# Attention and feed-forward kernel on one Trainium2 core: the order of its last outputs, the reading of its flag and the place of its short path

## The chip, the core and the metric

The kernel runs on one core of a Trainium2 chip. The core has five engines with instruction queues of their own: TensorE (PE, with its weight loads as PEld), VectorE (DVE), ScalarE (ACT), GpSimd (POOL) and SyncE (SP). [...] DMA transfers are issued here by SP, ACT and POOL. [...] The metric is the device time of one launch in microseconds (us); lower is better.

## What is computed

The input `x` has 32 batches of 64 rows of 512 columns. A cross-attention with 8 heads of 64 columns is added to it, and then a gated feed-forward with integer weights of 16 levels, each with a scale and a zero point for every group of 128 rows:

```
x = x + xattn(layernorm(x), ctx, ctx, Wq, bq, Wk, bk, Wv, bv, Wo, bo)
gate = silu(layernorm(x) @ ((gate_w - gate_z) * gate_s))    # 512 -> 1792
up   =      layernorm(x) @ ((up_w   - up_z)   * up_s)       # 512 -> 1792
x = x + (gate * up) @ ((down_w - down_z) * down_s)          # 1792 -> 512
```

All outputs are float32, 4 MB in all.

## The kernel before, in words

Two batches make a pair of 128 rows, so there are 16 pairs. Four pairs make a block, and there are four blocks, numbered `t` = 0 to 3. Each block's feed-forward works on columns: `hTh` and `hTl` hold the normalised rows turned over, split into a high and a low part so that each product is made of two matmuls. The 1792 inner columns are cut into 14 pieces (`FC`, index `f`). `gate_up(t, f)` makes one piece of gate and up in PSUM, with scalings on ACT (L643) between the groups, then silu (L646) and the product `h` (L649, DVE), which POOL splits into `hh` and `hl` (L659, L660). `down(t, f)` multiplies that piece into four PSUM tiles `pd`, one for each 128 output columns `l`, and DVE adds each to a running sum `y` in SBUF (L691). For the very last piece, ACT and DVE split `h` instead of POOL (L656, L657), and the last two pieces are accumulated in the same PSUM tiles after a scaling on ACT (L685).

**Rounds.** The main loop at L904 runs 118 rounds: 28 for a block and 6 more, since `down` lags six rounds (`LAG`) behind. In each round, `t, k = divmod(r, 28)`, and the loop traces one step of the gate and up lanes, some steps of the next block's attention, two steps of `down`, and side work. A scheduler orders what is traced, by its own estimate of when operands are ready and by trace order as priority. `tc.issue_after(ins)` pins what is traced inside it behind `ins` on the engine of `ins`. `tc.manual_schedule(engines={PE})` keeps PE's instructions in the order traced and together; `tc.high_priority()` inside it puts the rest of such a group ahead once its first instruction has been taken. `Attention.in_order` uses these two for the attention's groups of matmuls.

**Outputs of blocks 0 to 2.** `finish(t)` (L695) has four steps, two for each half of a block. One step loads the residual rows `r` of two pairs back from DRAM (L700, SP, 512 KB). The next turns `y` back into rows with eight transposes on PE into the two PSUM banks of `two_banks` (L705), adds `r` on DVE (L708) and sends two pairs of outputs (L709, SP, 512 KB). `two_banks` has one buffer, which the attention, `finish`, the bounds check and the last outputs share. The main loop takes a step of `finish(t)` in the rounds `k` = 7, 9 and 11 of block `t+1`, and the fourth at `k` = 5 of the block after that. Before the change, the fourth step of `finish(2)` therefore falls into round 117, the last one.

**Outputs of block 3.** `finish_last` (L712) transposes all four pairs (L720) into four PSUM banks, `py[0]` to `py[3]`, of which the last two are the banks of `two_banks`. DVE adds the residual `x` to pairs 0, 1 and 2 (L724). For pair 3, ACT copies the bank to SBUF as `y_last` (L727) and POOL adds the residual (L728). The four sends (L729, 256 KB each) are issued by SP for pairs 0 and 2 and by ACT for pairs 1 and 3. ACT's instructions are traced in the order: send of pair 1, copy of pair 3, send of pair 3.

**The flag.** The split-and-scale arithmetic is exact enough only within bounds on the scales and weights. `check_bounds` computes a one-word `flag` (L758) in round 106, at 406.7 us of the profiled execution. At L939, every engine loads the flag into a register and branches: non-zero leads to a long way, which computes the feed-forward again in plain form. With these inputs the flag is zero and the long way is never run. In the program before, the block of the long way stands right behind the branch, the block of the short way behind it, and the end of the program last. The long way has 286 instructions on SP, 469 on ACT, 509 on DVE, 2087 on PE and 29 on POOL. The short way only brings the semaphores to the values that the long way would have left: one wait-and-add on each of PE, DVE, ACT and POOL, for the engine's own work, and eight on SP, one for each semaphore that counts landed DMAs. So SP waits there until the last output has landed. The end of the program is twelve more waits on SP, and barriers of all engines.

Of the kernel before, what the change touches and what calls it, by code (L numbers as in the profile page):

```python
# [9 lines left out]
F32 = mybir.dt.float32  # L10
# [16 lines left out]
def kernel(  # L27
# [41 lines left out]
    nc = tc.nc  # L69
    B, D, L = x.shape  # L70
    I = gate_w.shape[1]
    P = 128
# [3 lines left out]
    LC = L // P  # L76
    NPAIR = B // 2
    PB = 4
    NBLK = NPAIR // PB
    TB = PB * P  # L80
    SET = 2
# [4 lines left out]
    o_rows = out.rearrange("(n b) d l -> (b d) n l", b=2)  # L86
# [7 lines left out]
    flag = keep.tile([1, 1], I32, tag="flag", name="flag")  # L94
    ident = keep.tile([P, P], F32, tag="ident", name="ident")
# [18 lines left out]
    with ExitStack() as fast:  # L114
# [204 lines left out]
        def top_steps():  # L319
# [9 lines left out]
            for piece in pieces:  # L329
# [3 lines left out]
                nc.gpsimd.tensor_tensor(total[:, :n], total[:, :n], square[:, :n], ALU.add)  # L333
                yield


        class Attention:

# [27 lines left out]
                flat = src.rearrange("p i l -> p (i l)")  # L366
                return flat.rearrange("p (n h d) -> p n h d", h=2, d=D)

            @contextmanager
            def in_order(self):  # L370


                with tc.manual_schedule(engines={mybir.EngineType.PE}), ExitStack() as ahead:
                    yield lambda: ahead.enter_context(tc.high_priority()) if self.n > 1 else None


            def stats(self):
# [215 lines left out]
        FINISH_AT = 7, 11  # L593
# [27 lines left out]
        h_hi, h_lo, y_sb, pd_two = {}, {}, {}, {}  # L621
# [73 lines left out]
        def finish(t: int):  # L695

            for a in range(0, PB, SET):
                p = t * PB + a
                r = rows.tile([P, SET, L], F32, tag="r", name=f"r_{p}")
                nc.sync.dma_start(r, x1_dram[:, p : p + SET, :])  # L700
                yield
                py = two_banks(f"py_{p}")
                for i in range(SET):
                    for l in range(LC):
                        nc.tensor.transpose(  # L705
                            py[:, i, ts(l, P)], y_sb[t, l][:, ts(a + i, P)], ident
                        )
                nc.vector.tensor_tensor(r, py, r, ALU.add)  # L708
                nc.sync.dma_start(o_rows[:, p : p + SET, :], r)  # L709
                yield  # L710

        def finish_last():  # L712

            t = NBLK - 1
            py = [ps_gu.tile([P, CW], F32, tag="gu", name=f"py_last_{i}") for i in range(2)]
            two = two_banks("py_last")
            py += [two[:, 0, :], two[:, 1, :]]
            for l in range(LC):
                for i in range(PB):
                    nc.tensor.transpose(py[i][:, ts(l, P)], y_sb[t, l][:, ts(i, P)], ident)  # L720
            for i in range(PB):
                r = xs[(t * PB + i) // SET][:, i % SET, :]
                if i < PB - 1:
                    nc.vector.tensor_tensor(r, py[i], r, ALU.add)  # L724
                else:
                    y = hid.tile([P, TB], F32, tag="g", name="y_last", bufs=2)
                    nc.scalar.copy(y, py[i])  # L727
                    nc.gpsimd.tensor_tensor(r, y, r, ALU.add)  # L728
                (nc.scalar if i % 2 else nc.sync).dma_start(o_rows[:, t * PB + i, :], r)  # L729


        def check_bounds():
# [57 lines left out]
        with (  # L790
# [9 lines left out]
            for p in range(PB):  # L800
                j, i = divmod(p, SET)
# [96 lines left out]
        ROUNDS = 2 * FC  # L898
        LAG = 6
        done = object()  # L900
        bounds = check_bounds()
        BOUNDS_AT = 3 * ROUNDS + FC + LC
        with ExitStack():
            for r in range(NBLK * ROUNDS + LAG):  # L904
                t, k = divmod(r, ROUNDS)
                if k == 0:
                    attend = attention_steps(t + 1) if t + 1 < NBLK else iter(())
                if k == LAG and t > 0:
                    finishing = finish(t - 1)
                next(lanes[0], done)  # L910
                advance(attend)
                if r >= LAG:
                    advance(downs)
                if r >= 2:
                    next(lanes[1], done)

                with ExitStack() as behind:
                    for ins in newest.values():
                        behind.enter_context(tc.issue_after(ins))
                    if r in (5, 13):  # L920
                        load_weights(*wide[(5, 13).index(r) + 2])
                    if r < ROUNDS:
                        advance(weights, 2 if r < 4 else 1 + r % 2)
                    else:
                        advance(tops, 1 + (r % 4 == 3))
                    if k in FINISH_AT or k + 2 in FINISH_AT:
                        advance(finishing)
                if r >= LAG:
                    advance(downs)
                if r == ROUNDS:  # L930
                    with tc.issue_after(newest["DVE"]):
                        last_quotients()
                if r in (BOUNDS_AT, BOUNDS_AT + 4):
                    with tc.issue_after(newest["DVE"]):
                        next(bounds, None)
        finish_last()


    with tc.If(nc.values_load(flag, min_val=0, max_val=1) != 0), ExitStack() as slow:  # L939
        const = slow.enter_context(tc.tile_pool(name="f_const", bufs=1))  # L940
        work = slow.enter_context(tc.tile_pool(name="f_work", bufs=2))
        ps = slow.enter_context(
            tc.tile_pool(name="f_ps", bufs=2, space=bass.MemoryType.PSUM)
        )
        wg = const.tile([P, KT, I], F32, tag="wg", name="f_wg")
        wu = const.tile([P, KT, I], F32, tag="wu", name="f_wu")
        wd = const.tile([P, FC, L], F32, tag="wd", name="f_wd")

        def dequantise(dst: bass.AP, w: bass.AP, z: bass.AP, s: bass.AP, n: int, name: str):
            w_sb = work.tile([P, CW], I32, tag="w", name=f"f_w_{name}")  # L950
            z_sb = work.tile([P, CW], I32, tag="z", name=f"f_z_{name}")
            s_sb = work.tile([P, CW], F32, tag="s", name=f"f_s_{name}")
            nc.sync.dma_start(w_sb[:, :n], w)
            nc.sync.dma_start(z_sb[:, :n], z.partition_broadcast(P))
            nc.sync.dma_start(s_sb[:, :n], s.partition_broadcast(P))

            nc.vector.tensor_tensor(dst, w_sb[:, :n], z_sb[:, :n], ALU.subtract)
            nc.vector.tensor_tensor(dst, dst, s_sb[:, :n], ALU.mult)

        for at, n in wide:  # L960
            c = slice(at, at + n)
            for g in range(KT):
                dequantise(wg[:, g, c], gate_w[ts(g, P), c], gate_z[g, c], gate_s[g, c], n, f"g{g}{at}")
                dequantise(wu[:, g, c], up_w[ts(g, P), c], up_z[g, c], up_s[g, c], n, f"u{g}{at}")
        for f in range(FC):
            dequantise(wd[:, f, :], down_w[ts(f, P), :], down_z[f, :], down_s[f, :], L, f"d{f}")

        for p in range(NPAIR):
            xp = work.tile([P, L], F32, tag="x", name=f"f_x_{p}")
            nc.sync.dma_start(xp, x1_dram[:, p, :])  # L970
            xn = work.tile([P, L], F32, tag="xn", name=f"f_xn_{p}")
            mv, rs = ln_stats(xp, f"s{p}")
            ln_scale(rs)
            ln_apply(xn, xp, mv, rs)
            ph = ps.tile([P, KT, P], F32, tag="ph", name=f"f_ph_{p}")
            for c in range(KT):
                nc.tensor.transpose(ph[:, c, :], xn[:, ts(c, P)], ident)
            hT = work.tile([P, KT, P], F32, tag="hT", name=f"f_hT_{p}")
            nc.scalar.copy(hT, ph)
            h_sb = work.tile([P, FC, P], F32, tag="h", name=f"f_h_{p}")  # L980
            for f in range(FC):
                pg = ps.tile([P, 2, P], F32, tag="gu", name=f"f_gu_{p}_{f}")
                for m, w in enumerate((wg, wu)):
                    for k in range(KT):
                        nc.tensor.matmul(
                            pg[:, m, :], w[:, k, ts(f, P)], hT[:, k, :], start=(k == 0), stop=(k == KT - 1)
                        )
                g_sb = work.tile([P, P], F32, tag="g", name=f"f_g_{p}_{f}")
                nc.scalar.activation(g_sb, pg[:, 0, :], AF.Silu)
                nc.vector.tensor_tensor(h_sb[:, f, :], g_sb, pg[:, 1, :], ALU.mult)  # L990
            pd = ps.tile([P, L], F32, tag="pd", name=f"f_pd_{p}")
            for f in range(FC):
                nc.tensor.matmul(pd, h_sb[:, f, :], wd[:, f, :], start=(f == 0), stop=(f == FC - 1))
            nc.vector.tensor_tensor(xp, pd, xp, ALU.add)
            nc.sync.dma_start(o_rows[:, p, :], xp)
# [52 lines left out]
```

## Time and profile before

| what | value |
|---|---|
| median of 4 runs | 442.38 us (441.8 to 444.09) |
| the profiled execution's own time | 442.91 us |
| its span, from first to last instruction | 440.8 us |
| time outside the span | 2.1 us |
| busy share of PE, DVE, ACT, POOL | 92%, 75%, 69%, 64% |
| mean granted TensorE clock | 0.990 |
| the last step of `finish(2)` on DVE (L708) | starts 429.23, takes 1.21 |
| sends of the four last pairs | 432.24, 432.84, 433.44, 435.40 |

"Busy" counts arithmetic; waits, register loads, branches and DMA issues are not in it. Matmuls overlap, so PE can be called busy while it still waits a little. Lines such as L939 in the profile are lines of the kernel before.

### The profile page before, as it was taken

To read this page: it belongs to the slowest core of one execution; us is meant where nothing else is said; L and a number is where in the kernel's file an instruction comes from. 1 tells how busy PE (TensorE), PEld (TensorE's weight loads), DVE (VectorE), ACT (ScalarE), POOL (GpSimd) and SP (SyncE) were. 2 spreads that over 40 slices of the span, in tenths; PEclk is the share of its full clock that TensorE was granted. 3 is DMA by queue.
4 is the path that set the end of the run, shared out by engine and by line. 5 is a ranking of instruction groups with operands and counts; after the bars stand their busy time and mean duration, and the time that the engine had idled before them with its cause. 6 is when DMAs were issued, how large, how long until landed. Compare 5 with 4: busy or idle time off the path is not lost.

```text
span 440.8 us, 10355 instructions
## 1 busy us (share of the span) xinstructions
PE 406.7 (92%) x4191; PEld 313.1 (71%) x4191; DVE 330.3 (75%) x514; ACT 306.2 (69%) x469; POOL 280.0 (64%) x292
## 2 busy tenths in 40 slices
PE   4768988989889999999999999989999999999991
PEld 3646656757668776877777787867778888887870
DVE  4988577897789875895779885895868646668682
ACT  2243887565967579766988589657887787777750
POOL 4384948754944546575788668765787878873311
PEclk9999989999999999999999999999999999999997
DMA  7299549197011200411010111400010022100004
GB/s 212 67 311 371 183 127 303 49 263 239 2 49 48 98 2 0 144 51 51 0 50 2 49 38 60 145 0 3 0 50 1 1 90 62 41 1 0 1 2 150
DMA packets 20912, 36.55 MB, mean 83 GB/s; under 512 B 1832, under 2 KB 7416, under 8 KB 20856
## 3 DMA queue, kind: packets, MB, share of 16 engines
q1 hardware_dynamic: 14056, 24.20, 16.6%
q0 software_dynamic: 6192, 11.01, 8.7%
q8 instruction: 35, 0.57, 0.6%
q10 hardware_dynamic: 608, 0.59, 0.4%
q14 instruction: 21, 0.17, 0.1%
HBM read 27.37 MB, written 8.42 MB: 81 GB/s over the span
## 4 chain that ended last, share of the span: by engine, by line
PE 51%; POOL 16%; DVE 13%; issue 11%; ACT 5%; DMA 2%; POOLq 0%; ACTq 0%; DVEq 0%
PE pu L633 14%; PE pg L633 14%; PE pd L678 7%; PE pd L681 6%; POOL hl L660 4%; POOL squares L333 3%; DVE y L691 3%; POOL squares L331 3%; POOL hh L659 2%; DVE xn_set L112 2%; DVE nd L301 2%; ACT pu L643 1%; POOL q_e_set L503 1%; ACT pg L643 1%; DMA x<-in_x_dram 1%
## 5 line engine op out<-in xcount | busy, mean ns | idle before, releaser
L691 DVE SCALAR_TENSOR_TENSOR y<-pd,s_all,y 128x512 f32<-128x512 f32 x204 | 150.2, 744 | 42.9 <-PE pd L681 39.9
L643 ACT ACTIVATE pg<-pg,s_q 128x512 f32<-128x512 f32 x168 | 111.6, 666 | 67.1 <-PE pg L633 65.7
L643 ACT ACTIVATE pu<-pu,s_q 128x512 f32<-128x512 f32 x168 | 111.1, 663 | 8.3 <-PE pu L633 7.3
L659 POOL CAST hh<-h 128x512 fp32r<-128x512 f32 x55 | 35.9, 652 | 97.7 <-DVE h L649 95.9
L678 PE MATMUL pd<-hh,nd 128*128 128x512 f32 x224 | 93.1, 416 | 3.0 <-DVE y L691 2.3
L633 PE MATMUL pg<-hTh,ng 128*128 128x512 f32 x224 | 90.3, 403 | 3.1 <-DVE hTl L576 1.6
L633 PE MATMUL pu<-hTh,nu 128*128 128x512 f32 x224 | 90.8, 406 | 1.5 <-POOL nu L310 1.4
L633 PE MATMUL pg<-hTl,ng 128*128 128x512 f32 x224 | 89.2, 398 | 0.0
L633 PE MATMUL pu<-hTl,nu 128*128 128x512 f32 x224 | 89.0, 397 | 0.0
L681 PE MATMUL pd<-hl,nd 128*128 128x512 f32 x224 | 88.6, 396 | 0.0
L660 POOL TENSOR_TENSOR hl<-h,hh 128x512 fp32r<-128x512 f32 x55 | 71.7, 1303 | 4.3
L649 DVE SCALAR_TENSOR_TENSOR h<-pu,s_all,g 128x512 f32<-128x512 f32 x56 | 41.8, 747 | 30.0 <-ACT g L646 18.1
L333 POOL TENSOR_TENSOR squares<-squares 128x512 f32<-128x512 f32 (+1 forms) x46 | 55.1, 1198 | 1.6
L678 PEld LDWEIGHTS pd<-hh,nd 128*128 128x128 f32 x224 | 42.0, 188 | 19.3 <-DVE y L691 5.9
L633 PEld LDWEIGHTS pg<-hTh,ng 128*128 128x128 f32 x224 | 42.4, 189 | 17.5 <-issue 3.0
L633 PEld LDWEIGHTS pu<-hTh,nu 128*128 128x128 f32 x224 | 42.3, 189 | 15.9 <-POOL nu L310 2.1
L633 PEld LDWEIGHTS pg<-hTl,ng 128*128 128x128 f32 x224 | 42.4, 189 | 9.4
L633 PEld LDWEIGHTS pu<-hTl,nu 128*128 128x128 f32 x224 | 42.4, 189 | 9.3
L646 ACT ACTIVATE g<-pg,s_all 128x512 f32<-128x512 f32 x56 | 38.9, 695 | 14.2 <-PE pg L633 12.7
L681 PEld LDWEIGHTS pd<-hl,nd 128*128 128x128 f32 x224 | 42.1, 188 | 7.7
L310 POOL TENSOR_TENSOR nu<-nu,z 128x512 fp32r<-128x512 f32 (+1 forms) x16 | 17.3, 1084 | 1.6 <-DMA nu<-in_L_ffn_up_w_dram 1.6
L310 POOL TENSOR_TENSOR ng<-ng,z 128x512 fp32r<-128x512 f32 (+1 forms) x16 | 16.5, 1040 | 1.8 <-DMA z<-z_dram 1.8
(293 smaller groups left out, 467.3 us busy)
## 6 DMA issues: line engine op xcount, KB each, us to landing
c_set<-in_ctx_dram SPq DMA_DIRECT2D x6, 512.0 KB
x<-in_x_dram SPq DMA_DIRECT2D x6, 512.0 KB
z<-z_dram SPq DMA_DIRECT2D x6, 512.0 KB
ng<-in_L_ffn_gate_w_dram POOLq DMA_DIRECT2D x3, 1024.0 KB, 6.1
nu<-in_L_ffn_up_w_dram POOLq DMA_DIRECT2D x3, 1024.0 KB, 8.0
x_dram<-x SPq DMA_DIRECT2D x6, 512.0 KB
r<-x_dram SPq DMA_DIRECT2D x6, 512.0 KB
out_dram<-r SPq DMA_DIRECT2D x6, 512.0 KB
```

The costliest lines, as they stand in the source:

```text
L310: nc.gpsimd.tensor_tensor(piece, piece.bitcast(F32), z16[:, m, g, :], ALU.subtract)
L331: nc.gpsimd.tensor_tensor(square[:, :n], piece, piece, ALU.mult)
L333: nc.gpsimd.tensor_tensor(total[:, :n], total[:, :n], square[:, :n], ALU.add)
L633: nc.tensor.matmul(acc, w[:, g, ts(f, P)], half[:, g, :], start=(g == 0 and half is hi), stop=(g == KT - 1 and half is lo), skip_group_che ...
L643: nc.scalar.activation(acc, acc, AF.Copy, scale=by)
L646: nc.scalar.activation(g_sb, acc, AF.Silu, scale=by)
L649: ins = nc.vector.scalar_tensor_tensor(h_sb, acc, by, g_sb, ALU.mult, ALU.mult)
L659: nc.gpsimd.tensor_copy(hh, h_sb)
L660: ins = nc.gpsimd.tensor_tensor(hl, h_sb, hh.bitcast(F32), ALU.subtract)
L678: nc.tensor.matmul(pd, w, h_hi[t, f], start=(t, f) != LAST, stop=False, skip_group_check=True)
L681: nc.tensor.matmul(pd, w, h_lo[t, f], start=False, stop=True, skip_group_check=True)
L691: ins = nc.vector.scalar_tensor_tensor(y, pd, by, y, ALU.mult, ALU.add)
```

## The change

There are four edits. (1) The group context of `Attention.in_order` becomes a free function `in_one_piece`, and `finish` puts its eight transposes into it, with priority after the first. (2) A constant `LAST_OUT` = 3·28 + 11 + 2 = 97 makes the main loop take the fourth step of `finish(2)` in round 97 instead of round 117. (3) In `finish_last`, ACT's copy of pair 3 is traced ahead of everything but the transposes, and ACT's sends are pinned behind it. (4) The flag is loaded ahead of `finish_last`; ACT's and POOL's instructions of `finish_last` are pinned behind their loads of it, and the conditional block is told to prefer the false arm, the short way, as the block that follows the branch.

```diff
+        @contextmanager
+        def in_one_piece(rush: bool = True):
+            with tc.manual_schedule(engines={mybir.EngineType.PE}), ExitStack() as ahead:
+                yield lambda: ahead.enter_context(tc.high_priority()) if rush else None
...
-            @contextmanager
             def in_order(self):
-                with tc.manual_schedule(engines={mybir.EngineType.PE}), ExitStack() as ahead:
-                    yield lambda: ahead.enter_context(tc.high_priority()) if self.n > 1 else None
+                return in_one_piece(self.n > 1)
...
                 py = two_banks(f"py_{p}")
-                for i in range(SET):
-                    for l in range(LC):
-                        nc.tensor.transpose(
-                            py[:, i, ts(l, P)], y_sb[t, l][:, ts(a + i, P)], ident
-                        )
+                with in_one_piece() as first_taken:
+                    for i in range(SET):
+                        for l in range(LC):
+                            nc.tensor.transpose(
+                                py[:, i, ts(l, P)], y_sb[t, l][:, ts(a + i, P)], ident
+                            )
+                            first_taken()
...
+            y = hid.tile([P, TB], F32, tag="g", name="y_last", bufs=2)
+            copied = nc.scalar.copy(y, py[PB - 1])
             for i in range(PB):
                 r = xs[(t * PB + i) // SET][:, i % SET, :]
                 if i < PB - 1:
                     nc.vector.tensor_tensor(r, py[i], r, ALU.add)
                 else:
-                    y = hid.tile([P, TB], F32, tag="g", name="y_last", bufs=2)
-                    nc.scalar.copy(y, py[i])
                     nc.gpsimd.tensor_tensor(r, y, r, ALU.add)
-                (nc.scalar if i % 2 else nc.sync).dma_start(o_rows[:, t * PB + i, :], r)
+                with tc.issue_after(copied.ins):
+                    (nc.scalar if i % 2 else nc.sync).dma_start(o_rows[:, t * PB + i, :], r)
...
+        LAST_OUT = (NBLK - 1) * ROUNDS + FINISH_AT[1] + 2
...
-                    if k in FINISH_AT or k + 2 in FINISH_AT:
+                    if k in FINISH_AT or k + 2 in FINISH_AT or r == LAST_OUT:
                         advance(finishing)
...
-        finish_last()
+        n_traced = len(nc.cur_bb.bb.instructions)
+        other = nc.values_load(flag, min_val=0, max_val=1)
+        with ExitStack() as behind:
+            for ins in nc.cur_bb.bb.instructions[n_traced:]:
+                if ins.engine in (mybir.EngineType.Activation, mybir.EngineType.Pool):
+                    behind.enter_context(tc.issue_after(ins))
+            finish_last()
...
-    with tc.If(nc.values_load(flag, min_val=0, max_val=1) != 0), ExitStack() as slow:
+    with tc.If(other != 0, preferred_fallthrough_block=False), ExitStack() as slow:
```

## The prediction

> **What bounds the kernel now.** I read the page first, then windows of the last rounds, the timeline of the last ten microseconds, and the instructions of the flag's line. The page:
>
> ```profile
> span 440.8 us, 10355 instructions
> PE 406.7 (92%) x4191; PEld 313.1 (71%) x4191; DVE 330.3 (75%) x514; ACT 306.2 (69%) x469; POOL 280.0 (64%) x292
> ...
> q8 instruction: 35, 0.57, 0.6%
> q14 instruction: 21, 0.17, 0.1%
> ```
>
> PE bounds the run, so work moved about beside PE is free and work moved onto PE is not. The two instruction queues fetch code: 35 packets of 16 KB on q8, 21 of 8 KB on q14. The windows show PE full in block 3, with room on DVE and POOL:
>
> ```profile
> 380.00:400.00 20.00, 20.00 (x87) 15.78 (x86) 14.93 (x30) 15.64 (x26) 13.52 (x14) 1.00 0.00 1
> 400.00:420.00 20.00, 20.00 (x88) 15.72 (x86) 14.13 (x21) 14.80 (x25) 7.09 (x8) 1.00 0.00 0
> ```
>
> The columns after the window are its length and then busy time of PE, PEld, DVE, ACT and POOL. The change acts on the tail:
>
> ```profile
> 429.23 1.21 DVE L708 TENSOR_TENSOR r<-py,r 128x1024 f32<-128x1024 f32 x1
> 430.36 0.74 DVE L691 SCALAR_TENSOR_TENSOR y<-pd,s_all,y 128x512 f32<-128x512 f32 x1
> 431.52 1.89 DVE L724 TENSOR_TENSOR x<-py_last,x 128x512 f32<-128x512 f32 x3 [0.42 <-PE py_last L720]
> 432.24 1.53 SPq L729 DMA_DIRECT2D out_dram<-x  x2
> 433.44 0.59 ACT L727 COPY y_last<-py_last 128x512 f32<-128x512 f32 x1 [5.91 <-DVE x L724]
> 434.11 1.26 POOL L728 TENSOR_TENSOR x<-y_last,x 128x512 f32<-128x512 f32 x1 [12.52 <-DMA out_dram<-x]
> 435.40 0.34 ACTq L729 DMA_DIRECT2D out_dram<-x  x1
> ...
> L939 SPq EVENT_SEMAPHORE  x8: 17/17/17, 437.0 to 438.8; - x8
> L939 PEldq COMPARE_BRANCH  x1: 4357/4357/4357, 432.2 to 432.2; - x1
> L939 SPq COMPARE_BRANCH  x1: 45/45/45, 433.8 to 433.8; - x1
> L939 POOLq COMPARE_BRANCH  x1: 54/54/54, 435.0 to 435.0; - x1
> L939 POOLq EVENT_SEMAPHORE  x1: 17/17/17, 435.4 to 435.4; - x1
> L939 ACTq COMPARE_BRANCH  x1: 58/58/58, 436.3 to 436.3; - x1
> L939 ACTq EVENT_SEMAPHORE  x1: 17/17/17, 439.9 to 439.9; - x1
> ```
>
> The reader is to see two things. DVE's add for block 2 (L708) stands between block 3's sums and their last member. And a branch over the long way is dear: SP branches at 433.82 and does its next instruction at 436.98, 3.16 us later; ACT goes from 436.32 to 439.85 (3.53), PE takes 4.36, while POOL, whose long way has only 29 instructions, takes 0.36 (435.04 to 435.40). On SP this lies beside the outputs' flight. The trace's semaphore events put the last landing of pair 3 at 438.69. SP takes it at 438.71 and needs 0.13 for two more waits, then twelve waits of the program's end, 0.062 each. The last of those stands 0.31 for ACT's late semaphore; with ACT in time, the end would be 440.52 in place of 440.81. So ACT's branch is worth 0.29, and the landing rules.
>
> **The block 2 step, moved from round 117 to 97.** Eight transposes start 0.109 apart (260.10 to 260.86 in an earlier group). Rounds 89 and 93 stand at 355.75 and 367.82 (transposes), so a round is 3.02 and round 97 is near 379.9. PE is full there: +0.87. DVE's 1.21 fits into its 5.07 idle us of that window; with no such cover it adds up to 1.21. The residual load (L700) is issued at 373.1, nearly 7 us ahead, where a 512 KB send took 2.8 (430.47 to 433.26): 0; if late, the add and the send wait, not PE. The moved send on SP has only the flag's load (406.8) behind it: 0. In the tail L708 goes: the three sums from 427.20 end at 429.31, so the last `y` starts at 429.23, as L708 did, not 430.36: −1.13. The twelve transposes that waited for L708's bank are done by then. Net so far −0.26: last `y` ends at 430.84 instead of 431.10. Keeping the other groups together costs nothing: all five already run 0.11 apart. If priority puts a group ahead of its free bank, PE stands; the nearest row is PE's wait for L708's bank, 0.69.
>
> **The copy first.** Pair 3's last transpose ends 0.71 after the last `y` (431.81), so ACT can copy at 431.60 (430.84 + 0.71 + 0.05) instead of 433.44. With 0.59, a hop of 0.07 and POOL's 1.26 the add ends at 433.52 and the send leaves at 433.55, not 435.40: −1.85. POOL's add now runs beside DVE's; `hl` took 1.30 under a busy DVE, so +0.04 at most. Behind the copy on ACT stand the sends of pairs 1 and 3; pair 1 waits for DVE until 432.58 anyway, after the copy ends at 432.19: 0. The other sends move by −0.26, to 431.98, 432.58 and 433.18.
>
> **The flag early.** ACT's load (0.47) falls between 427.5, its last scaling, and 431.6; POOL's (0.90) after 421.6: 0, without cover +0.47 and +0.90. PE's (0.96) and DVE's (0.82) are not pinned; I leave them last, as now. Ahead of PE's transposes it would cost +0.96 at most. SP's already stands at 406.8.
>
> **The short way behind the branch.** The long way must then stand elsewhere. The only other place that leaves the rest in order is between the short way and the program's end, so the short way ends in a jump over the long way, as far as the jump of before. The stall is not removed; it moves behind the short way's waits. For PE, DVE and ACT that stays hidden: ACT sends at 433.55, is through 0.34 later, and with 3.53 is done by 437.6. For SP it does not: its jump now comes after the last landing. The price is bounded by POOL's 0.36 and PE's 4.36; I take SP's own row, 3.16, the same engine and distance.
>
> [...]
>
> **Landing.** Without laggards, 15 of 16 parts of pairs 0, 1 and 2 landed by 434.27, 434.95 and 435.64, some 2.03 after the send and 0.68 apart; so pair 3 would be in at 436.06 (431.98 + 2.03 + 3 × 0.68). But each pair's last part was late (436.54, 437.22, 437.81) while code packets were fetched (433.9 to 435.2). The fetches stay among the sends, as PE and DVE jump right after their work. Pair 2 took 4.38 from send to landing: 437.56 now, and pair 3 0.64 behind it, 438.20. By pair 3's own row, 3.30, it is 436.85. I take the middle, 437.5; ends 436.06 and 438.2.
>
> **Sum.** Landing 437.5, two waits and the take-up 0.15, jump 3.16, twelve waits 0.74, hand-over 0.06, closing barriers 0.87 (439.94 to 440.81): 442.5 against 440.8, so +1.7. The profiled execution took 442.91, 2.1 around its span, and lies 0.53 above the median; on its own time I get 444.6, on the median's scale 444.1.
>
> **The rivals.** *First, no jump on SP's path* (faster): the end follows the short way directly, or the target is already fetched. For it: POOL's 0.36 shows a cheap jump. Against it: the distance. Then 437.5 + 0.15 + 0.74 + 0.06 + 0.87 = 439.3 with laggards, 437.9 without (no jumps, no fetches among the sends): −1.5 to −2.9, taken at −2.6, 439.8. It decides where the stall falls under 3.16 − 1.7 = 1.4. *Second, the moved step disturbs block 3*: DVE's 1.21 delays `y` sums, PE waits for `pd` banks (8 such waits, 5.9 us in all, before), or a group stands for its bank: 0.69 to 1.9 on top, 444.8 to 446.0, 445.5 with the jump. Against it: after L708 at 369.04 the windows show no gap on PE. *Third, the jump stays but laggards go*: landing 436.06, +0.2, 442.6; it needs the fetches to miss the sends.
>
> **How the numbers follow.** 0.5% is 2.2 us, about what a measurement of this kernel can tell from no change. The jump with its landing between the two ends: 0.70 (third rival included with 0.15), own range 442.4 to 445.3 from landing 436.06 to 438.2 and a stall of 3.1 to 3.5; about a third of it lies above 444.6. First rival 0.17, range 439.3 to 441.0, two thirds of it below 440.2. Second rival 0.13, nearly all above 444.6. Faster 0.12; slower 0.23 + 0.11 = 0.34; within 0.54. For 8 in 10 the range takes in both: 439.5 to 445.4.
>
> **What would show it.** Right: the flag line's eight SP waits now start soon after 433.8, as soon as SP branches, and end with the last landing; then some 3 us without any SP instruction before the closing waits; ACT's copy starts ahead of both its sends, near 431.6; no L708 after 382. Wrong: closing waits directly behind the last landing (first rival), or PE gaps near 380 (second). The prediction fails by most if the place of the long way is not as I argue.

## The result, and the profile after

| | median | range | runs |
|---|---|---|---|
| before | 443.24 us | 441.22 to 444.98 | 78 |
| after | 444.38 us | 442.56 to 446.56 | 52 |

The ratio of after to before is 1.0031, with a 95% interval of 1.0023 to 1.0040: slower by 1.0 to 1.8 us, which is within the 0.5% that the prediction called no change. The profiled execution of after took 445.28 us, its span is 443.18, so 2.10 lies around the span as before.

In the change, line 708 became 713 (DVE's add), 709 became 714, 720 became 725, 724 became 732, 727 became 728, 728 became 734, 729 became 736, 649 became 652 and 691 became 694. Line 939 was split: the loads of the flag are at 946, the branch and the short way at 954. The end of the program is 1058.

The top of the page of after, the lines that answer those of before:

```profile
span 443.2 us, 10359 instructions
PE 406.2 (92%) x4191; PEld 311.5 (70%) x4191; DVE 330.8 (75%) x514; ACT 306.0 (69%) x469; POOL 280.3 (63%) x292
...
q8 instruction: 35, 0.57, 0.5%
q14 instruction: 22, 0.17, 0.1%
```

Nothing was added to or taken from the arithmetic; the span is 2.4 us longer with the same work, and 0.83 of that is drift, which is taken off below. The windows of block 3 after:

```profile
380.00:400.00 20.00, 20.00 (x91) 16.22 (x90) 14.99 (x28) 14.62 (x24) 13.39 (x13) 1.00 0.07 27
400.00:420.00 20.00, 20.00 (x87) 15.47 (x86) 14.60 (x23) 15.49 (x26) 7.64 (x8) 1.00 0.00 1
```

The first window has 91 matmuls in place of 87, and a DMA share of 0.07 in place of 0.00. That is the moved step with its transposes and its send. PE has no gap; the step pushes the rest of block 3 back by its own length.

To compare ends, one correction is needed. The executions drift apart in the first 140 us: after's products `h` (L652) are 0.80 later than before's at 125.4 us and still 0.83 at 380.4, and the executions in the table below stand between −0.7 and +1.3 us to the one of before. I read the drift at one of DVE's products `h` in block 3, and the cost of the moved step at the next one. Before, then after:

```profile
380.40 0.75 DVE L649 SCALAR_TENSOR_TENSOR h<-pu,s_all,g 128x512 f32<-128x512 f32 x1 [0.50 <-ACT g L646]
...
384.60 0.75 DVE L649 SCALAR_TENSOR_TENSOR h<-pu,s_all,g 128x512 f32<-128x512 f32 x1 [0.50 <-ACT g L646]
```

```profile
381.24 0.75 DVE L652 SCALAR_TENSOR_TENSOR h<-pu,s_all,g 128x512 f32<-128x512 f32 x1 [0.49 <-ACT g L649]
...
386.32 0.75 DVE L652 SCALAR_TENSOR_TENSOR h<-pu,s_all,g 128x512 f32<-128x512 f32 x1 [0.49 <-ACT g L649]
```

The first `h` is 0.83 later, the next 1.72. So the moved step costs 0.88 (1.715 less 0.834). Times "on before's scale" below have the drift taken off.

In the views a "q" behind an engine's name (SPq, ACTq) marks register loads, branches, semaphore waits and DMA issues. Arithmetic of the same engine can lie beside them: DVE's load of the flag before (0.82 from 431.9) lies beside its three adds (431.52 to 433.41). The timeline of the tail of after:

```profile
429.54 2.15 DVE L694 SCALAR_TENSOR_TENSOR y<-pd,s_all,y 128x512 f32<-128x512 f32 x3
...
431.08 1.53 PE L725 MATMUL py_last<-ident,y 128*128 128x128 f32 x12 [0.41 <-DVE y L694]
432.32 1.89 DVE L732 TENSOR_TENSOR x<-py_last,x 128x512 f32<-128x512 f32 x3 [0.64 <-PE py_last L725]
432.65 0.59 ACT L728 COPY y_last<-py_last 128x512 f32<-128x512 f32 x1 [3.38 <-PE py_last L725]
433.04 1.53 SPq L736 DMA_DIRECT2D out_dram<-x  x2
433.31 1.27 POOL L734 TENSOR_TENSOR x<-y_last,x 128x512 f32<-128x512 f32 x1 [10.01 <-ACT y_last L728]
433.64 2.04 ACTq L736 DMA_DIRECT2D out_dram<-x  x2
```

The copy now runs beside DVE's adds, and ACT has issued its second send 1.07 us after it began at 434.61. On before's scale pair 3 leaves at 433.78 instead of 435.40. Now the instructions of the branch's line, and SP's closing waits, of after (durations in ns, then the first and last start in us):

```profile
L954 SPq EVENT_SEMAPHORE  x8: 17/17/17, 434.7 to 438.9; - x8
L954 PEldq COMPARE_BRANCH  x2: 90/2062/4033, 432.3 to 432.8; - x2
...
L954 SPq COMPARE_BRANCH  x2: 38/44/49, 434.6 to 438.9; - x2
L954 ACTq COMPARE_BRANCH  x2: 38/48/57, 435.7 to 435.9; - x2
```

```profile
L1058 SPq EVENT_SEMAPHORE  x14: 17/28/28, 441.5 to 443.1; - x14
```

Each engine now has two branches at this line: one into the short way, which costs SP 0.10 (434.62 to 434.72), and one out of it, over the long way. SP's eight waits begin right behind the first, at 434.72, and end behind the last landing (438.70 by the trace's semaphore events; SP takes it at 438.72). SP's second branch is at 438.92, its next instruction at 441.55. For those 2.63 us no engine does any work. PE's jump (432.81 to 436.90), DVE's (434.34 to 437.88) and ACT's (435.89 to 438.50) lie ahead of that, hidden.

So the change sends the last pair 1.62 us sooner, the last landing comes only 0.83 sooner (437.87 on before's scale against 438.69), and the end comes 4.48 behind the landing instead of 2.11: −0.83 + 2.37 = +1.54 in the traces. What became of the missing 0.8 of the earlier send is a question for the experiments.

### The profile page after: what moved, and what is told of

It reads as the page before. It is cut to its first block, busy times and chain, and to the rows that moved or that the text cites. A ratio compares the mean times of both kernels' runs of the same rounds, so it can differ in the third digit from the quotient of the medians.

```text
span 443.2 us, 10359 instructions
## 1 busy us (share of the span) xinstructions
PE 406.2 (92%) x4191; PEld 311.5 (70%) x4191; DVE 330.8 (75%) x514; ACT 306.0 (69%) x469; POOL 280.3 (63%) x292
## 4 chain that ended last, share of the span: by engine, by line
PE 48%; POOL 18%; DVE 12%; issue 11%; DMA 5%; ACT 4%; POOLq 0%; SPq 0%; DVEq 0%; ACTq 0%
PE pu L636 13%; PE pg L636 13%; PE pd L681 7%; PE pd L684 6%; POOL hl L663 4%; DMA nd<-in_L_ffn_down_w_dram 4%; POOL squares L333 3%; DVE y L694 3%; POOL squares L331 3%; POOL hh L662 2%; DVE nd L301 2%; DVE xn_set L112 1%; POOL q_e_set L506 1%; DMA x<-in_x_dram 1%; POOL nu L310 1%
## 5 line engine op out<-in xcount | busy, mean ns | idle before, releaser
L652 DVE SCALAR_TENSOR_TENSOR h<-pu,s_all,g 128x512 f32<-128x512 f32 x56 | 41.9, 747 | 29.3 <-ACT g L649 18.6
```

What stands on the lines that cost most here:

```text
L652: ins = nc.vector.scalar_tensor_tensor(h_sb, acc, by, g_sb, ALU.mult, ALU.mult)
```

## The experiments

All ratios are to runs of the kernel before on the same chip, taken together with it. Each experiment has 12 runs, except "no long way" (6) and "long first, short jump" (11). The other columns are read from one trace of each kernel, on before's scale and each rounded on its own, in the order run.

| kernel | ratio | 95% interval | cost in block 3 | pair 3 sent | last landing | end − landing | end |
|---|---|---|---|---|---|---|---|
| before | 1 | | | 435.40 | 438.69 | 2.11 | 440.81 |
| after | 1.0031 | 1.0023 to 1.0040 | 0.88 | 433.78 | 437.87 | 4.48 | 442.35 |
| long way first | 1.0011 | 0.9990 to 1.0032 | 0.88 | 433.75 | 437.92 | 2.61 | 440.53 |
| short way first, alone | 1.0042 | 1.0023 to 1.0062 | 0 | 435.41 | 437.94 | 4.38 | 442.32 |
| block 2's step, alone | 0.9992 | 0.9971 to 1.0012 | 0.88 | 435.35 | 438.62 | 1.83 | 440.44 |
| copy first, alone | 0.9988 | 0.9968 to 1.0008 | 0 | 433.80 | 438.52 | 1.83 | 440.35 |
| short jump on SP | 0.9973 | 0.9953 to 0.9994 | 0.87 | 433.73 | 437.89 | 2.05 | 439.94 |
| no long way | 0.9917 | 0.9894 to 0.9941 | 0.87 | 433.95 | 436.47 | 0.97 | 437.44 |
| step back, off DVE | 0.9990 | 0.9972 to 1.0007 | 0 | 433.01 | 437.83 | 2.04 | 439.87 |
| long first, short jump | 0.9937 | 0.9919 to 0.9956 | 0.88 | 433.78 | 437.14 | 1.83 | 438.97 |
| the same, sends on SP | 0.9995 | 0.9972 to 1.0018 | 0.87 | 434.73 | 438.68 | 1.83 | 440.51 |

Two things are in the ratios and not in these ends. The time outside the span is 2.10 to 2.13 us on average before, after and in the first four experiments, but 1.80 to 1.85 in the last five, which all have a shorter long way on SP; so 0.25 to 0.31 of what the last five gain lies outside the span, and no run shows why. And the mean granted clock was 0.9935 in the runs of "no long way" and of "long first, short jump", against 0.9897 and 0.9887 in before's runs beside them. A straight line through after's own runs has the span 2 us shorter for 0.01 more clock, so a part of these two ratios may be clock.

My theory: SP's jump behind the short way is what costs, and the rest of the change gains. Its rivals: a landing or a block 3 made worse by the other edits.

**The long way first, the rest as after.**

```diff
-    with tc.If(other != 0, preferred_fallthrough_block=False), ExitStack() as slow:
+    with tc.If(other != 0), ExitStack() as slow:
```

> The changed kernel without its wish for the short way behind the branch; all other edits stay. Theory (SP's jump over the long way, 2.63 us in the changed kernel, 438.92 to 441.55, was moved behind the last landing): SP jumps at its branch again, beside the flight of the outputs, and the closing waits follow the last landing at once, so 2.6 us less than the changed kernel; ACT sends 0.8 us earlier than before, so its jump of 3.5 us ends in time. Ratio to the kernel before 1.0031 - 2.6/443 = 0.997 (0.996 to 0.998). Rival (the regrouped transposes and the moved step disturb the rounds, the jump is hidden as it was): the time stays at 1.003.

Measured 442.92 us, ratio 1.0011 (0.9990 to 1.0032). The ratio alone does not tell this kernel from after. In the trace the stall behind the landing went, as expected, but the end comes 1.82 sooner than after's, not 2.6. The branch's line in this kernel:

```profile
L954 SPq EVENT_SEMAPHORE  x8: 17/17/17, 438.4 to 438.9; - x8
...
L954 SPq COMPARE_BRANCH  x1: 45/45/45, 434.0 to 434.0; - x1
L954 ACTq COMPARE_BRANCH  x1: 58/58/58, 434.2 to 434.2; - x1
...
L954 ACTq EVENT_SEMAPHORE  x1: 17/17/17, 438.6 to 438.6; - x1
```

SP jumps at 433.99, while the outputs are still on their way, and needs 4.41 us; ACT needs 4.36 from 434.20. When SP arrives at 438.40, the last output has landed 0.40 ago (438.00), and SP still has eight waits of the short way and twelve closing ones to pass. The jump is no fixed price: it took SP 2.5 to 2.6 us with nothing else moving (this section's next kernel, and after), and 2.97 to 4.41 among the sends.

**The short way first, alone (the kernel before with only the layout changed).**

```diff
-    with tc.If(nc.values_load(flag, min_val=0, max_val=1) != 0), ExitStack() as slow:
+    with tc.If(nc.values_load(flag, min_val=0, max_val=1) != 0, preferred_fallthrough_block=False), ExitStack() as slow:
```

> The kernel before with one edit: the short way is wished for behind the branch. Theory: SP's jump comes behind its waits for landed outputs; the last landing stays near 438.7, and 2.6 to 3.2 us without any SP instruction follow it; less the 0.29 us by which ACT was late before: 2.3 to 2.9 us longer, ratio 1.005 to 1.007. Rival (the jump costs nothing where it stands, the loss is elsewhere): 1.000 or, as ACT is no longer late, 0.9993.

Measured 444.87 us, ratio 1.0042 (1.0023 to 1.0062). The layout by itself makes the kernel slower, and by as much as the whole change does. It is less than the 1.005 to 1.007 that I expected, as the last landing came 0.75 sooner (437.94 against 438.69) where I had let it stay.

```profile
L939 SPq EVENT_SEMAPHORE  x8: 17/17/17, 433.2 to 437.4; - x8
...
L939 SPq COMPARE_BRANCH  x2: 38/44/49, 433.1 to 437.5; - x2
```

```profile
L1043 SPq EVENT_SEMAPHORE  x14: 17/28/28, 440.0 to 441.6; - x14
```

SP's second branch is at 437.48, its next instruction at 440.01: 2.53. A second reading is in the table: here pair 3 is sent at 435.41, as late as in the kernel before, and lands at 437.94. After sends it at 433.78 and lands it at 437.87. The send that is 1.6 us earlier lands 0.07 earlier.

**Block 2's last step in round 97, alone.**

```diff
+        LAST_OUT = (NBLK - 1) * ROUNDS + FINISH_AT[1] + 2
...
-                    if k in FINISH_AT or k + 2 in FINISH_AT:
+                    if k in FINISH_AT or k + 2 in FINISH_AT or r == LAST_OUT:
```

> The kernel before with one edit: the last step of block 2's outputs is taken in round 97. Theory: PE is full there, so the rounds behind it move by 0.87 us (8 transposes of 0.109), and the tail gives back 1.13 (the add no longer stands between the sums): net -0.26 us, ratio 0.9994 (0.998 to 1.001). Rival (the moved step disturbs block 3 further, by DVE's add of 1.21 us or a bank that isn't free): rounds behind it move by 1.5 to 2.8 us, ratio 1.001 to 1.004.

Measured 442.70 us, ratio 0.9992 (0.9971 to 1.0012): as expected, no difference that these runs can tell. The trace has 0.88 more in block 3, and the last `y` ends 0.26 sooner on before's scale (430.84 against 431.10), near −1.13 + 0.88.

**The copy of pair 3 first, alone.**

```diff
+            y = hid.tile([P, TB], F32, tag="g", name="y_last", bufs=2)
+            copied = nc.scalar.copy(y, py[PB - 1])
...
-                    y = hid.tile([P, TB], F32, tag="g", name="y_last", bufs=2)
-                    nc.scalar.copy(y, py[i])
...
+                with tc.issue_after(copied.ins):
+                    (nc.scalar if i % 2 else nc.sync).dma_start(o_rows[:, t * PB + i, :], r)
```

> The kernel before with one edit: ACT copies the last pair ahead of its sends. Theory: the copy starts at 431.9 instead of 433.44 and the last send leaves 1.6 us earlier, near 433.8; the last landing moves less, as it follows pair 2's latest part (437.8) by some 0.64: -0.2 to -1.6 us at the landing, and ACT's jump ends 1.6 us earlier, so its lateness of 0.29 goes as well. -0.5 to -1.9 us, ratio 0.9957 to 0.999. Rival (the landing is set by parts that are delayed by code fetches, not by the time of the send): -0.3 us, 0.9993.

Measured 442.43 us, ratio 0.9988 (0.9968 to 1.0008). The interval takes in most of my theory's range and the rival's 0.9993; the trace decides. Pair 3 is sent 1.60 us sooner, and lands 0.17 sooner: the earlier send is eaten by late landing, as the rival had it. Where does it go? Of each transfer's 16 parts, one or a few come late. In this trace pair 0 leaves at 432.21, 15 parts are in by 434.24, the last at 436.61. In the kernel with only the layout changed, the first packet of code on q8 begins at 433.51, as pair 0 lands: there pair 0 has hardly a late part (433.61, the last at 433.83). That pointed to the fetches of code that run among the sends.

**The jump on SP made short.** SyncE's long way is long because it issues the weight loads; here ScalarE issues them. The computation is the same.

```diff
-            nc.sync.dma_start(w_sb[:, :n], w)
-            nc.sync.dma_start(z_sb[:, :n], z.partition_broadcast(P))
-            nc.sync.dma_start(s_sb[:, :n], s.partition_broadcast(P))
+            nc.scalar.dma_start(w_sb[:, :n], w)
+            nc.scalar.dma_start(z_sb[:, :n], z.partition_broadcast(P))
+            nc.scalar.dma_start(s_sb[:, :n], s.partition_broadcast(P))
```

> The changed kernel, but the weight loads of the long way are issued by ScalarE instead of SyncE: SyncE's long way, which its jump after the last landing crosses, shrinks from 286 to 61 instructions, ScalarE's grows from 469 to 699. The short way is unchanged, the long way never runs with these inputs. My theory (the stall after the landing is the fetch of code that lies far away): SyncE's stall falls from 2.63 us to 0.2 to 0.5 us (GpSimd's jump over 29 instructions took 0.16 us in the changed kernel); ScalarE's jump of 2.6 us still ends under the last landing; the kernel ends 2.1 to 2.4 us sooner than the changed one, a ratio to the kernel before of 0.998 (0.997 to 0.999). Rival (any jump at that place costs some 2.6 us, whatever its length): the stall stays at 2.5 us and the ratio at 1.003.

Measured 441.96 us, ratio 0.9973 (0.9953 to 0.9994). The theory held in the trace; the ratio takes in 0.25 from outside the span as well.

```profile
L954 SPq EVENT_SEMAPHORE  x8: 17/17/17, 433.6 to 437.8; - x8
...
L954 SPq COMPARE_BRANCH  x2: 38/44/49, 433.5 to 437.9; - x2
```

```profile
L1058 SPq EVENT_SEMAPHORE  x14: 17/28/28, 438.0 to 439.6; - x14
```

The branch is at 437.85, the next instruction at 438.04: 0.19 us over 61 instructions, where after took 2.63 over 286. Landing and block 3 are those of after (437.89 and 437.87), so the 2.41 between the two ends are this jump. Two packets of 8 KB of code, from 439.37 to 440.32, lie in after's stall; none lies in this one. ScalarE's jump, now over 699 instructions, took 2.85 (434.80 to 437.65), where it took 2.61 over 469: 230 more instructions added 0.24.

**No long way.** The body of the long way is one pair copied.

```diff
-        def dequantise(dst: bass.AP, w: bass.AP, z: bass.AP, s: bass.AP, n: int, name: str):
...
-        for p in range(NPAIR):
+        for p in range(1):
...
-            nc.vector.tensor_tensor(xp, pd, xp, ALU.add)
```

> The changed kernel with the long way cut down to the copy of one pair; left out is the whole recomputation in FP32 that would run if the flag were not zero, which it never is with these inputs. No engine then has a long jump, and no code is fetched while the outputs are sent. My theory (the late last sixteenth of each output is a transfer that stands behind fetches of code on the same DMA engine): SyncE's stall of 2.63 us goes and the last part of the last output lands with its fellows, at 437.4 us instead of 438.70 us in the changed kernel's trace: together 3.9 us less than the changed kernel, a ratio to the kernel before of 0.994 (0.993 to 0.996). Rival (the late sixteenth has nothing to do with fetches of code): only the 2.6 us of the stall go, ratio 0.9975.

Measured 439.27 us, ratio 0.9917 (0.9894 to 0.9941): more than my theory had it, and the trace's end is 4.91 sooner than after's instead of 3.9. No code is fetched in the tail, and no part is late: the last two of each pair's 16 parts land within 0.05 us of each other, and pair 3 is in 2.52 after its send, against 4.09 in after. The share of the DMA engines in use, in tenths, and what they moved, in 40 slices of 0.16 us, first for after (432.9 to 439.3), then for this kernel (432.0 to 438.4):

```profile
DMA  0000067999998999997339998311100040100000
GB/s 0 0 0 0 0 102 269 371 384 371 359 346 282 371 397 384 371 384 295 115 128 397 371 397 307 115 51 51 38 26 26 26 128 0 51 0 0 0 0 0
```

```profile
DMA  0000007999999999998999940000000000000000
GB/s 0 0 0 0 0 0 282 397 384 397 333 384 371 397 410 371 397 397 333 397 358 410 397 141 0 0 0 0 0 0 0 0 0 0 0 0 0 0 0 0
```

In after, a thin trickle, mostly of 26 to 51 GB/s, runs on for some 1.4 us after the bulk is through: that is the late parts. Here the transfers stop at once. Against after the landing is 1.40 sooner. The rest, 3.51, lies behind the landing: 2.63 of jump, and 0.88 that I had left out. This kernel's branches are passed before the last sends, so SP waits for the landings among the closing waits, and by the last landing all the others are passed. In after fourteen waits of about 0.062 still follow the landing. That this layout differs in that too is a side effect of the edit; the late parts are read from the landings alone.

So the late parts come with the long way. The DMA packets of after's trace show how they end: pair 2's last sixteenth is eight packets of 2 KB, one every 0.080 us from 436.97 to 437.62, and pair 3's is eight more, from 437.62 to 438.27, on another queue but with no gap between. So these late parts wait in one line. My estimate of what put that line behind is a packet of code on the same DMA engine: one of 16 KB ran from 433.70 to 435.30, and pair 0's last part landed 1.80 behind its others. But the trace does not tell which of the 16 engines a packet used, and no run separates this from other effects of a jump.

**The step back in round 117, but off DVE** (on top of the short jump on SP).

```diff
+                    ins = nc.scalar.activation(pd, pd, AF.Copy, scale=d_last[:, l : l + 1])
+                    scaled.append(ins.ins)
...
-                nc.vector.tensor_tensor(r, py, r, ALU.add)
+                if p == NPAIR - PB - SET:
+                    with ExitStack() as behind:
+                        for ins in scaled:
+                            behind.enter_context(tc.issue_after(ins))
+                        nc.scalar.copy(place["c"], py)
+                    nc.gpsimd.tensor_tensor(r, place["c"], r, ALU.add)
+                else:
+                    nc.vector.tensor_tensor(r, py, r, ALU.add)
...
-                    if k in FINISH_AT or k + 2 in FINISH_AT or r == LAST_OUT:
+                    if k in FINISH_AT or k + 2 in FINISH_AT:
```

> The kernel with the short jump on SyncE, and block 2's last outputs back in round 117, as in the kernel before, but with their add taken off VectorE: ScalarE copies the transposed pair out of PSUM behind its last four scalings, GpSimd adds it to the rows. My theory (the moved step costs block 3 0.88 us, and its only cost at the end was its place on VectorE ahead of the last y): the last y ends 0.9 us sooner than in the kernel with the short jump alone, at about 430.8 us, and the kernel ends 0.9 us sooner, a ratio to the kernel before of 0.996 (0.995 to 0.9975). Rival (TensorE's 8 transposes or ScalarE's copy of 1.2 us delay the tail just as much, or GpSimd's add of some 2.5 us delays its last add): the gain is between 0 and 0.3 us, ratio 0.998.

Measured 442.72 us, ratio 0.9990 (0.9972 to 1.0007). The 0.88 in block 3 is gone and the last `y` ends 0.7 sooner (430.10 on before's scale, against 430.81). The end is not sooner: 439.87 against 439.94. The rival named the right outcome for the wrong reason. PE, ACT and POOL delay nothing, but the output's 512 KB do; the timeline, with the line numbers of this kernel:

```profile
429.63 2.36 POOL L720 TENSOR_TENSOR r<-c_set,r 128x1024 f32<-128x1024 f32 x1 [7.00 <-ACT c_set L719]
...
432.01 0.39 SPq L723 DMA_DIRECT2D out_dram<-r  x1
...
432.51 1.52 SPq L745 DMA_DIRECT2D out_dram<-x  x2
```

Block 2's send leaves 0.50 ahead of pair 0's. Of pair 0, 15 parts are in 3.17 after its send (435.68), where 2.03 was enough without it. In the tail the DMA engines were full (9 in tenths, above), and the output that was sent there was paid for there. This is what moving the step to block 3 buys, where the DMA share is 0.07 and 0.00 in after's two windows, the step's own send included.

**The long way first with the short jump on SP**, that is, the first and the fifth experiment together.

```diff
-    with tc.If(other != 0, preferred_fallthrough_block=False), ExitStack() as slow:
+    with tc.If(other != 0), ExitStack() as slow:
...
-            nc.sync.dma_start(w_sb[:, :n], w)
+            nc.scalar.dma_start(w_sb[:, :n], w)
...
```

> The kernel with the weight loads of the long way on ScalarE, in the layout of the kernel before: the long way stands first, and every engine jumps over it after its last send, while the outputs land. My theory (the stall is code that lies far away; SyncE's is short over 61 instructions, ScalarE's long over 699): SyncE stands at its closing waits by 434.5 us and waits only for the last landing, at some 438.0 us as in the kernel with the long way first and long jumps; ScalarE's jump after its last send ends at about 438.6 us, as there, and is now the last thing. The end comes 1.0 to 1.3 us sooner than there (440.61 us), about 0.4 us sooner than with the short jump after the landing; ratio to the kernel before 0.996 (0.9945 to 0.998). Rival (the longer long way makes ScalarE's jump longer, in the measure of 699 to 469 instructions, some 2 us): the end is at 441.5 us, ratio 1.002.

Measured 441.01 us, ratio 0.9937 (0.9919 to 0.9956): faster than before, more than I expected, and by the two ratios some 0.9% faster than after.

```profile
L954 SPq EVENT_SEMAPHORE  x8: 17/17/17, 435.3 to 438.6; - x8
...
L954 SPq COMPARE_BRANCH  x1: 45/45/45, 435.1 to 435.1; - x1
L954 ACTq COMPARE_BRANCH  x1: 58/58/58, 435.4 to 435.4; - x1
...
L954 ACTq EVENT_SEMAPHORE  x1: 17/17/17, 438.9 to 438.9; - x1
```

SP branches at 435.08 and waits from 435.26 on (0.19). The last landing is at 438.43, SP takes it at 438.44, and nothing but waits follows. ACT's jump took 3.51 over 699 instructions (435.43 to 438.95), where it took 4.36 over 469 with the long way first and long jumps, and ends under SP's closing waits, so the rival, a jump that grows with the distance, falls. The landing itself came 0.77 sooner than with the long way first and long jumps; that is one trace each, and I had not expected it. The traces give an end 1.84 sooner than before's; with 0.29 from outside the span that is 0.48%. The runs' interval is 0.44 to 0.81%.

**The same, with all four sends on SP.**

```diff
-                    (nc.scalar if i % 2 else nc.sync).dma_start(o_rows[:, t * PB + i, :], r)
+                    nc.sync.dma_start(o_rows[:, t * PB + i, :], r)
```

> The same, and SyncE issues all four of the last outputs instead of taking turns with ScalarE, so that ScalarE can jump as soon as it has copied the last pair, 2 us sooner. SyncE's issues (0.33 to 0.41 us each, 0.6 us apart) follow one another without a queue. My theory: ScalarE's jump ends by 436.6 us, no jump is left at the end, and the last landing (437.4 to 438.0 us) sets it; the end is 0.2 to 0.6 us sooner than with the sends shared, ratio to the kernel before 0.995 (0.9935 to 0.997). Rival (ScalarE's fetch of code now stands among all four outputs, and one queue lands later than two): the last landing is 0.5 to 1 us later and the gain is gone, ratio 0.996 to 0.998.

Measured 442.89 us, ratio 0.9995 (0.9972 to 1.0018): the gain is gone.

```profile
L736 SPq DMA_DIRECT2D out_dram<-x x4: 337/517/1242, 432.3 to 434.9; - x4
```

ACT's jump was done by 434.66, as my theory had it, but SP's second issue took 1.24 us instead of 0.36, so the next send left at 434.10 instead of 433.40 on before's scale, and the last landing is 1.54 later than with the sends shared. The rival had it, and more so. While ACT jumps, packets of code at 432.86 and 434.20 now lie among the sends. The lengthened issue lies beside a code packet of q8, the queue with packets of 16 KB, that took 1.29 (432.55 to 433.84); in after the issue of 1.07 lies beside one of 1.59. In the kernel without a long way all four issues take 0.33 to 0.36.

## Why the prediction was right

The prediction was right on the direction of the trace, the mechanism and the size: +1.7 us forecast, +1.54 in the traces, 1.0 to 1.8 by the runs' ratio. Part of the close agreement in microseconds (444.1 and 444.38) is chance: the forecast was scaled to a median of 442.38, and the larger set of runs of before has 443.24.

| term of the sum | predicted | measured, on before's scale |
|---|---|---|
| moved step, in block 3 | +0.87 | +0.88 |
| last `y` ends | 430.84 | 430.85 |
| copy of pair 3 starts | 431.60 | 431.82 |
| sends of pairs 0, 1, 2, 3 | 431.98, 432.58, 433.18, 433.55 | 432.21, 432.81, 433.40, 433.78 |
| last landing | 437.5 (436.06 to 438.2) | 437.87 |
| SP's jump behind it | 3.16 | 2.63 |
| end | 442.5 | 442.35 |

- *The layout* was right: the short way ends in a long jump, on SP behind the landing. The layout alone (a stall of 2.53), the change without it (no jump behind the landing) and the shortened jump (0.19) show it from three sides.
- *The stall's row* was right in kind and 0.53 too large. SP's 3.16 came from a jump among the sends; behind the landing, with no output in flight, it took 2.53 and 2.63. Over 61 instructions SP took 0.19; no run has a jump of SP between these two lengths, so where it turns dear is not shown.
- *The twelve transposes* were not "done by then". DVE adds the four last `y` in the order 0, 2, 1, 3, and PE turns them in the order 0, 1, 2, 3. So PE waits for the third sum until 431.08 (430.25 on before's scale) and still has eight transposes before the last four: the copy came 0.22 later than I had it, and all sends with it. Nor did twelve wait for L708's bank before: six had been started by 429.53.
- *The flag early* was put at 0, and nothing else shows: the last `y` ends at 430.85, and at 430.84 with block 2's step alone. No run has this edit by itself.
- *The landing* was chosen as the middle of 436.06 and 438.2 and came 0.37 later. The lower end rested on a reading that was off: by 434.95 and 435.64 not 15 parts of pairs 1 and 2 had landed, but 14 and 13. The laggards stayed, as the prediction had it, and the kernel without a long way puts their price at 1.40. The late landing (+0.37) and the smaller stall (−0.53) nearly cancelled, and that is luck: without it the end would have been off by more than 0.15.
- *ACT's lateness of 0.29* went, as forecast: the ends of the two kernels with one edit alone and the long way first come 1.83 behind the landing, before's 2.11.
- *The rivals.* The first (no jump on SP's path) is what the shortened jump made, and it was worth less than I gave it: the end came 0.87 sooner than before's in the trace (439.94) and by the ratio 0.3 to 2.1, not 1.5 to 2.9. Its sum was 439.3 with laggards; the landing came 0.39 later than 437.5, and a near jump of 0.19 was left. The second (a disturbed block 3) did not happen: the cost was the transposes and nothing more. The third (no laggards) needed the long way to go.

What the prediction did not see is how little its −1.85 for the copy is worth at the landing. It let the landing come 1.2 sooner (437.5 against 438.69); 0.83 came, and the two kernels with the short way first, with and without the earlier send, differ there by 0.07 alone. Where the long way stands first, the copy alone gained 0.17. Yet the layout alone gained 0.75 at the landing (437.94), and the other edits without it 0.77 (437.92). The gains do not add up, and these are single traces; so the landing term was nearly right for another reason than the forecast's, and what sets the landing stays open.

## What to carry to other kernels

Preferring a block as fallthrough did not make its jump go away (2.53 to 2.63 us on SP, behind the landing); ask where the other block now lies, and which engine crosses it when nothing is left to hide it. The jump was dear here where it crossed many of the engine's own instructions (on SP 2.53 to 4.41 us over 286, 0.19 over 61), so count instructions engine by engine, and give the long stretch to an engine that has time to jump. And before an output is sent earlier, look at what else the DMA engines carry at that moment: here, most likely, code for the jumps, and in one experiment a neighbour's 512 KB, took back what an earlier send had gained.

## What the hardware showed that I had not expected

- Once a jump was far, its price depended on the traffic more than on the distance: SP over 286 instructions 2.53 and 2.63 in quiet, 2.97 to 4.41 among the sends; ACT over 469 instructions 2.53 to 4.36, with its long way grown to 699 or about as many 2.73 to 4.08. Near jumps took 0.16 (POOL, 29 instructions, in after) and 0.19 (SP, 61). POOL's 0.36 in before bounds its jump only from above: it ends at 435.40, right behind POOL's own add (435.37), for which the short way waits.
- A DMA issue of some 0.34 us took 1.07 on ACT (after) and 1.24 on SP (all sends on SP) while code was being fetched; I saw it beside packets of 16 KB on q8 that took 1.29 to 1.62 us, where the others of these tails took 0.88 to 1.38. Which of the two holds up the other is not shown.
- One of a transfer's 16 parts landed up to 2.4 us behind the other 15 (436.61 against 434.24 in the kernel with the copy alone), and no part was more than 0.05 us behind the one before it in the kernel without a long way, where no code was fetched.
